# Row turns as whole-array transposes in other groups, with a different home for the row maxima

## The chip, the cores and the metric

The kernel runs on one NeuronCore of one Trainium2 chip. The metric is the device time of that core in microseconds (us). The kernel before takes 3599.44 us, the median of three runs between 3599.09 and 3600.59 us.

The core has five engines with a queue of instructions each. TensorE (PE in the profile, with PEld for its loads of stationary weights) multiplies matrices and writes only to PSUM[...]. VectorE (DVE), ScalarE (ACT) and GpSimd (POOL) work element by element; SyncE (SP) issues most DMAs. An engine takes its queue in order; between engines, semaphores hold an instruction until what it needs is there.

## The reference

One transformer block in float32 with adaptive layer norm, over x of 8 batches x 1024 rows x 256 columns, and then a mixture of 8 experts:

```python
h = _layernorm(x) * (1 + ca) + sa               # ca, sa, ga ...: from c, one row per batch
proj = einsum('bpv,havn->bhapn', h, w_qkv)      # 16 heads of 64: q, k, v
scores = einsum('bhqn,bhkn->bhqk', q, k) / 8
attn = softmax(scores, axis=-1)                 # exact: the row's maximum is subtracted
x = x + ga * (einsum('bhqk,bhkn->bhqn', attn, v) as rows of 1024) @ w_o
h = _layernorm(x) * (1 + cb) + sb
logits = h @ router_w + router_b                # 8 experts
scores = softmax(logits)
G, idx = top_k(scores.T, 512)                   # each expert takes its 512 best rows
eo = relu(h[idx] @ w1 + b1) @ w2 + b2
x = x + gb * scatter_add(eo * G at idx)
```

## The kernel before, in words

**Units and groups.** Attention is cut into 128 units: one batch (8), one pair of heads (8) and one half of the 512 queries (2). A unit's scores stand with keys on the partitions: eight chunks `c` of 128 keys, each a PSUM tile `s` of 128 x 2 x 512 (two banks), made by `scores_mm`. The main loop (line 732) runs in groups `g` of two chunks, four groups to a unit; `gm` is `g % 4`, and this text calls `gm` 0, 1, 2, 3 the first to fourth group. ScalarE copies a chunk to SBUF (`scores_out`, line 376) and VectorE takes the running maximum `top` over chunks (line 381; none for chunk 0, so the first group has one such operation and the others two).

**The maximum of a unit.** At the end of the fourth group `max_turn` (line 383) turns `top` by eight transposes into a tile `tt`, which comes from the same pool of two score tiles, `ps_s`. `split_max` (line 392) reduces it to one negated maximum per query (line 396), and four small VectorE operations (lines 401 to 404) split that into three bf16 parts. They work in `nm`, a corner of `tt` itself: so `tt` is in use until line 404. In the next group `max_rows` turns the parts to rows, and a group later `max_spread` spreads them over all partitions (`less`).

**The lag.** Five groups behind, `subtract` (line 426) adds `less` to a chunk and `exp_of` (line 429) takes the exponential; one group later `values_mm` (line 438) multiplies by v, and GpSimd adds the chunks for the denominator (`add_up`, lines 454 and 457).

**A group's order.** In each group the loop emits: the list "load" of that group (DMAs), in second groups `max_spread`, the subtractions, the two chunks of scores, list "m1" (projections q, k, v, and `max_rows` in first groups), list "post", the exponentials, `values_mm`, `add_up`, in a fourth group `max_turn` and `split_max`, then list "pool" (GpSimd work) and list "m2". Each engine's queue has its part of this order. The lists are filled beforehand by `at(g, list, function, ...)` (line 247).

**One shared bank.** Projections, `max_rows`, denominators and everything in "m2" use one PSUM bank, the tag `mm` of `ps_m`: each user waits for the one before to be evicted.

**The tasks around the change.** For batches 1 to 7, `ln_task` loads 256 rows (four groups ahead), takes statistics (two ahead, list "post", on VectorE), normalises (one ahead, on GpSimd) and turns them in `ln_out` (list "m2"): 8 matmuls against the identity, each with half the array's columns (lines 302 to 309), and two evictions by VectorE (line 311). Batch 0 is turned by 128 x 128 transposes, two at a time, each pair evicted by ScalarE (lines 291 to 301). For each 128 rows of attention's output, `out_proj` multiplies by w_o and `out_add` (VectorE) adds the residual and takes statistics, `out_norm` (GpSimd, next group) normalises; for each pair of these, `out_turn` (line 576) turns 256 rows, again with half-array matmuls (line 585), one ScalarE copy (line 590), `out_route` computes logits, `out_exp` (ScalarE) and `out_score` (VectorE, lines 622 to 626) the softmax over experts, `out_store` stores the rows.

**Where they stand.** `free_slot(g, True)` (line 651) gives the next untaken fourth group, `free_slot(g)` the next untaken group that is neither first nor fourth. `ln_out`, `out_proj` and `out_turn` all take fourth groups: 4, 8 and 4 of the 16 in a batch, so that from unit 20 on each fourth group has one of them behind its `max_turn`. `out_route` then falls in a second group, `out_exp` in the third, `out_score` in the fourth.

The last batch's output (lines 771 to 823) and the experts (from line 826) follow the main loop; only `out_turn` there belongs to the change.

Of the kernel before, what the change touches and what calls it, by code (L numbers as in the profile page):

```python
# [37 lines left out]
P = 128  # L38
# [4 lines left out]
def adaln_block(  # L43
# [29 lines left out]
    scale = 1.0 / N**0.5  # L73
# [4 lines left out]
    ident = const.tile([P, P], F32, name="ident")  # L78
# [17 lines left out]
    modT = const.tile([P, 2 * KC, B], F32, name="modT")  # L96
# [36 lines left out]
    ps_m = attn.enter_context(tc.tile_pool(name="ps_m", bufs=1, space=PSUM))  # L133
# [33 lines left out]
    for i in range(2):  # L167
        t = work.tile([P, NT // 2, D], F32, tag="p", name=f"x_first{i}", bufs=PB)
# [73 lines left out]
    hTs, mods, qks, vs, oTs = {}, {}, {}, {}, {}  # L242
# [4 lines left out]
    def at(g, where, f, *args):  # L247
        steps.setdefault((g, where), []).append((f, args))
# [37 lines left out]
    def ln_out(b, t):  # L286
        if t == 0:
            hTs[b] = work.tile([P, KC, S], F32, tag="hT", name=f"hT{b}")
        xt = ln_x.pop((b, t))[0]
        pt = bank([P, KC, 2 * P], f"ptx{b}_{t}", (b, t) in ((0, 0), (0, 1)))  # L290
        if b == 0:
            for k in range(KC):
                for i in range(2):
                    nc.tensor.transpose(
                        pt[:, k, i * P : (i + 1) * P], xt[:, i, k * P : (k + 1) * P], ident
                    )
                nc.scalar.activation(
                    hTs[b][:, k, 2 * t * P : (2 * t + 2) * P], pt[:, k, :], AF.Identity,
                    bias=modT[:, k, b : b + 1], scale=modT[:, KC + k, b : b + 1],
                )  # L300
            return
        for k in range(KC):
            for i in range(2):
                for m in range(2):
                    c0 = k * P + m * N
                    nc.tensor.matmul(
                        pt[m * N : (m + 1) * N, k, i * P : (i + 1) * P],
                        xt[:, i, c0 : c0 + N], ident, start=True, stop=True,
                    )
        for k in range(KC):  # L310
            nc.vector.tensor_scalar(
                hTs[b][:, k, 2 * t * P : (2 * t + 2) * P], pt[:, k, :],
                modT[:, KC + k, b : b + 1], modT[:, k, b : b + 1],
                op0=ALU.mult, op1=ALU.add,
            )

    def ln_task(b, t, g):
        at(g - 4, "load", ln_load, b, t)
        at(g - 2, "post", ln_stats, b, t)
        at(g - 1, "pool", ln_norm, b, t)  # L320
        at(g, "m2", ln_out, b, t)
# [67 lines left out]
                    turned[u][:, 4 * j + t, :], top[:, j, t * P : (t + 1) * P], ident  # L389
                )  # L390

    def split_max(u):

        tt = turned.pop(u)
        nm = tt[:, :2, :8]
        nc.vector.tensor_reduce(nm[:, 0, :], tt, AX.X, ALU.max, negate=True)  # L396
# [7 lines left out]
        nc.vector.tensor_sub(part[2], rest, part[1])  # L404
# [171 lines left out]
    def out_turn(pool, b, t, tag="mm"):  # L576

        n = f"{b}_{t}"
        pt = pool.tile([P, 2, KC, P], F32, tag=tag, name=f"pth{n}")
        for i in range(2):  # L580
            h2 = o_h[b, t + i]
            for k in range(KC):
                for m in range(2):
                    c0 = k * P + m * N
                    nc.tensor.matmul(
                        pt[m * N : (m + 1) * N, i, k, :], h2[:, c0 : c0 + N], ident,
                        start=True, stop=True,
                    )
# [57 lines left out]
        )  # L646


    taken = set()

    def free_slot(g, behind=False):
        while g in taken or g % 4 == 0 or behind != (g % 4 == 3):
            g += 1
        taken.add(g)
        return g
# [9 lines left out]
    for b in range(B):  # L665
        for p in range(NP):
            P0 = 8 * (b * NP + p)
            for i, g in enumerate((-7, -6, -5, -2)):
                if P0:
                    at(P0 + g, "m1", qk_task, b, p, i)  # L670
            if p % 2 == 0:
                for t, g in enumerate((-9, -3, -1, 5)):
                    if P0 or g > 0:
                        at(P0 + g, "m1", v_task, b, p // 2, t)
            if (b, p) == (B - 1, NP - 1):
                continue

            at(P0 + 17, "load", den_load, b, p)
            at(P0 + 18, "post", den_inv, b, p)
            at(P0 + 19, "load", den_spread, b, p)  # L680
            at(P0 + 20, "pool", den_mul, b, p)
        if b + 1 < B:
            if b + 2 < B:
                for t in range(NT // 2):
                    ln_task(b + 2, t, free_slot(64 * (b + 1) + 39 + 4 * t, True))
            for t in range(NT):
                g = free_slot(64 * (b + 1) + 19 + 4 * t, True)
                at(g - 2, "load", out_load, b, t)
                at(g, "m2", out_proj, ps_m, b, t)
                at(g + 1, "pool", out_norm, b, t)  # L690
                if t % 2:
                    g = free_slot(g + 2, True)
                    at(g, "m2", out_turn, ps_m, b, t - 1)
                    g = free_slot(g + 1)
                    at(g, "m2", out_route, ps_m, b, t - 1)
                    at(g + 1, "post", out_exp, b, t - 1)
                    at(g + 2, "post", out_score, b, t - 1)
                    at(g + 3, "pool", out_store, b, t - 1)
    for u in range(NSU):
        at(4 * u + 4, "m1", max_rows, u)  # L700
        if u < NSU - 1:
# [8 lines left out]
    with tc.manual_schedule():  # L710
# [20 lines left out]
        g = -1  # L731
        while g < 4 * NSU + LAG or steps:
            u, gm = divmod(g, 4)
            run(g, "load")
            if gm == 1 and 0 < u <= NSU:
                max_spread(u - 1)
            u1, gm1 = divmod(g - LAG + 1, 4)
            late = [(u1, 2 * gm1 + i) for i in range(2) if 0 <= u1 < NSU]

            for uc in late[: 1 if gm == 3 else 2]:  # L740
                subtract(*uc)
            if 0 <= u < NSU:
# [24 lines left out]
            run(g, "m2")  # L767
            g += 1


        b = B - 1
# [85 lines left out]
    with tc.tile_pool(name="search", bufs=2) as se, tc.tile_pool(  # L857
        name="pos", bufs=1
    ) as po_, tc.tile_pool(name="se_ps", bufs=2, space=PSUM) as sps, tc.tile_pool(
        name="pos_ps", bufs=1, space=PSUM  # L860
    ) as pps:
        for dst, pattern, mult in (
# [3 lines left out]
            i = po_.tile(list(dst.shape), I32, name=f"i_{dst.name}")  # L866
# [32 lines left out]
        for s in range(15):  # L899
            bit = 28 - 2 * s  # L900
            cnt = se.tile([P, 3], F32, tag="cnt", name=f"cnt{s}")
            for k in range(3):
# [3 lines left out]
                    op0=ALU.is_ge, op1=ALU.add, accum_out=cnt[:, k : k + 1],  # L906
# [226 lines left out]
```

## Time and profile before

| | |
|---|---|
| median of the runs shown | 3599.44 us |
| the profiled execution | 3597.83 us |
| its span, first to last instruction | 3596.1 us |
| mean granted TensorE clock | 0.983 |
| busy: PE / PEld / DVE / ACT / POOL | 96% / 40% / 80% / 68% / 74% |
| PE idle before L367 (scores) | 34.0 us |
| L306, `ln_out`'s half-array matmuls (28 tasks) | 30.6 us busy |
| L585, `out_turn`'s (32 tasks) | 39.2 us busy |
| L388, `max_turn`'s transposes (128 units) | 139.9 us busy |

The page lists, for each line and engine, the count, busy time, mean duration and the idle time of the engine before it. The timeline gives instructions in order of time, runs of the same one merged: start, duration, engine, line, output <- inputs, count, and in brackets the idle time of the engine and what ended it. A float32 matmul stands as two records (two passes), a transpose as one. Ends of matmuls are modelled, and neighbours overlap on the PE; the time that a block takes on the PE is read from its start to the start of the next block.

Attention runs to about 3205 us of the span, the last batch's output and routing to about 3272 us; then come the search for each expert's rows and the experts.

### The profile page before, as it was taken

The page shows a single profiled execution, that of the slowest core. Times are in us where ns is not written, and L with a number is a line of the kernel's source. Part 1 is how long each engine was busy: PE and PEld are TensorE (multiplying, and loading weights), DVE is VectorE, ACT ScalarE, POOL GpSimd, SP SyncE. Part 2 cuts the span into 40 slices and gives each one's busy share as a digit, 9 for nine tenths or more (in the row PEclk, how much of TensorE's full clock was granted, in tenths as well). Part 3 has the DMA queues.
Part 4 walks back from the last instruction along what each step waited for, and adds up shares of the span by engine and source line. Part 5 has one row for each costly group of instructions (what it writes and reads, how often), then busy time and mean ns, then how long its engine had stood idle before and what let it go on. Part 6 is the DMA issues. An engine that isn't in the chain of part 4 may idle for free. (4 is left out here: it accounts for less than half of the span.)

```text
span 3596.1 us, 54368 instructions
## 1 busy us (share of the span) xinstructions
PE 3450.2 (96%) x20718; PEld 1454.7 (40%) x20718; DVE 2859.3 (80%) x3618; ACT 2438.7 (68%) x2996; POOL 2652.1 (74%) x1537
## 2 busy tenths in 40 slices
PE   7999999999999999999999999999999999993898
PEld 3333333343433434334433343344433434442566
DVE  5888888888888888888888888988888888867432
ACT  4777777777777777777777777777777777750111
POOL 2778778888888887978788888887888788752233
PEclk9999999999999999999999999999999999995899
DMA  3020012011130112111211112111211112133342
GB/s 78 13 42 31 25 32 67 30 45 45 51 59 29 50 57 56 34 40 45 66 53 31 48 50 63 31 42 53 59 44 44 41 44 63 46 92 129 93 101 43
DMA packets 189653, 185.40 MB, mean 52 GB/s; under 512 B 48952, under 2 KB 167240, under 8 KB 189264
## 3 DMA queue, kind: packets, MB, share of 16 engines
q1 hardware_dynamic: 173616, 160.29, 16.3%
q0 software_dynamic: 7168, 12.72, 1.8%
q10 hardware_dynamic: 8608, 8.92, 0.8%
q8 instruction: 163, 2.67, 0.3%
q14 instruction: 98, 0.80, 0.1%
HBM read 127.06 MB, written 63.21 MB: 53 GB/s over the span
## 5 line engine op out<-in xcount | busy, mean ns | idle before, releaser
L457 POOL TENSOR_TENSOR acc<-acc,p 128x1024 f32<-128x1024 f32 x762 | 1805.3, 2369 | 362.4 <-ACT p L429 329.1
L376 ACT COPY p<-s 128x1024 f32<-128x1024 f32 x1024 | 995.8, 1018 | 419.1 <-PE s L367 412.1
L426 DVE TENSOR_TENSOR p<-p,less 128x1024 f32<-128x1024 f32 x1024 | 1206.7, 1210 | 32.6 <-PE less L423 30.1
L381 DVE TENSOR_TENSOR top<-top,s 128x1024 f32<-128x1024 f32 x768 | 936.8, 1220 | 276.3 <-ACT p L376 236.0
L429 ACT ACTIVATE p<-p 128x1024 f32<-128x1024 f32 x1024 | 1041.7, 1057 | 73.7 <-DVE p L426 73.3
L367 PE MATMUL s<-qk,qk 64*128 64x512 f32 x4096 | 1024.7, 612 | 34.0 <-DVE parts L404 31.0
L438 PE MATMUL av<-p,v 128*64 128x512 f32 x4096 | 967.2, 593 | 1.8 <-ACT oT L447 1.8
L367 PEld LDWEIGHTS s<-qk,qk 64*128 64x128 f32 x4096 | 358.8, 186 | 527.5 <-issue 240.9
L332 PE MATMUL pq<-hT,wq 128*64 128x512 f32 x2048 | 498.5, 608 | 2.7 <-ACT v L354 2.1
L438 PEld LDWEIGHTS av<-p,v 128*64 128x64 f32 x4096 | 280.6, 137 | 461.4 <-issue 366.2
L454 POOL TENSOR_TENSOR acc<-p,p 128x1024 f32<-128x1024 f32 x127 | 301.6, 2375 | 178.1 <-ACT p L429 178.1
L332 PEld LDWEIGHTS pq<-hT,wq 128*64 128x64 f32 x2048 | 124.8, 136 | 342.2 <-issue 210.8
L349 PE MATMUL pv<-wq,hT 128*64 128x256 f32 x2048 | 249.3, 386 | 0.7 <-ACT qk L337 0.7
L1053 ACT ACTIVATE h<-ph,b_sb 128x512 f32<-128x512 f32 (+1 forms) x72 | 46.0, 639 | 263.5 <-PE ph L1049 263.5
L396 DVE TENSOR_REDUCE tt<-tt 128x8 f32<-128x1024 f32 x128 | 157.4, 1230 | 69.9 <-PE tt L388 69.8
L548 PE MATMUL po<-wo,ot 128*64 128x256 f32 x1792 | 205.7, 382 | 0.0
L349 PEld LDWEIGHTS pv<-wq,hT 128*64 128x64 f32 x2048 | 135.7, 136 | 153.2 <-issue 65.9
L381 DVE TENSOR_TENSOR top<-p,s 128x1024 f32<-128x1024 f32 x128 | 155.8, 1217 | 14.0 <-ACT p L376 14.0
L388 PEld LDWEIGHTS tt<-ident,top 128*128 128x128 f32 x1024 | 109.6, 140 | 106.6 <-DVE top L381 105.8
L519 POOL TENSOR_TENSOR oT<-oT,rb 128x1024 f32<-128x1024 f32 x63 | 150.0, 2380 | 3.7 <-DMA rb<-rden_d 3.7
L548 PEld LDWEIGHTS po<-wo,ot 128*64 128x64 f32 x1792 | 123.5, 137 | 66.1 <-issue 9.4
L388 PE MATMUL tt<-ident,top 128*128 128x128 f32 x1024 | 139.9, 280 | 2.6 <-DVE top L381 2.6
(169 smaller groups left out, 2293.4 us busy)
## 6 DMA issues: line engine op xcount, KB each, us to landing
rb<-rden_d SPq DMA_DIRECT2D x128, 256.0 KB
oT_d<-oT SPq DMA_DIRECT2D x62, 512.0 KB
ot<-oT_d SPq DMA_DIRECT2D x56, 512.0 KB
rows_d<-row SPq DMA_DIRECT2D x64, 132.0 KB
rows_d<-gb_d SPq DMA_DIRECT2D x8, 1024.0 KB
w<-in_L_ffn_w_dram ACTq DMA_DIRECT2D x8, 1024.0 KB
w<-in_L_ffn_w_dram SPq DMA_DIRECT2D x8, 1024.0 KB
lnx<-in_L_attn_inputs_dram SPq DMA_DIRECT2D x28, 256.0 KB
```

Source lines behind the costliest of these rows:

```text
L332: nc.tensor.matmul(pq[m * N : (m + 1) * N, :], wq_of(k, a, 2 * p + m), hTs[b][:, k, sl], start=(k == 0), stop=(k == KC - 1),)
L349: nc.tensor.matmul(pv[m * N : (m + 1) * N, i, :], hTs[b][:, k, t0 : t0 + N], wq_of(k, 2, 4 * g, 4), start=(k == 0), stop=(k == KC - 1),)
L367: nc.tensor.matmul(ps[:, j, :], kt[r, c * P : (c + 1) * P], qt[r, h * QB : (h + 1) * QB], start=True, stop=True,)
L376: nc.scalar.copy(probs[u, c], ps)
L381: nc.vector.tensor_tensor(tops[u], probs[u, 0] if c == 1 else tops[u], ps, ALU.max)
L388: nc.tensor.transpose(turned[u][:, 4 * j + t, :], top[:, j, t * P : (t + 1) * P], ident)
L426: nc.vector.tensor_tensor(probs[u, c], probs[u, c], less[u], ALU.add)
L429: nc.scalar.activation(probs[u, c], probs[u, c], AF.Exp)
L438: nc.tensor.matmul(avs[u][j * N : (j + 1) * N, :], v[:, c, hh * N : (hh + 1) * N], pT[:, j, :], start=(c == 0), stop=(c == NT - 1),)
L454: nc.gpsimd.tensor_tensor(sums[u], pts[0], pts[1], ALU.add)
L457: nc.gpsimd.tensor_tensor(sums[u], sums[u], pt, ALU.add)
L548: nc.tensor.matmul(po[m * N : (m + 1) * N, :], ot[:, p, m * N : (m + 1) * N], wo[:, p, :], start=(p == 0), stop=(p == NP - 1),)
```

## The change

- `ln_out` uses one path for all batches: four 128 x 128 transposes into the bank, then two ScalarE evictions. For batch 0 all four transposes now stand ahead of both evictions; for the others half-array matmuls and VectorE evictions are gone.
- `out_turn` uses four transposes too.
- `split_max(u, busy)`: where the fourth group has an `out_proj` behind it (the set `covered`, 56 of 128 units), `nm` stays in `tt`. In the other 72, `nm` is a tile of the shared bank `mm`.
- `ln_out` moves to third groups, 30, 34, 42 and 46 of the batch before (with its load, statistics and normalisation moving along: the statistics stand in first groups 28, 32, 40, 44). `out_proj` stands in fourth groups 19, 23, 31, 35, 43, 47, 55, 59; `out_turn` three groups after the second of a pair (third groups), `out_route` six after (second), `out_exp` seven after (third), `out_score` nine after (first), `out_store` ten after (second).

```diff
@@ ln_out
-        if b == 0:
-            for k in range(KC):
-                for i in range(2):
-                    nc.tensor.transpose(...)
-                nc.scalar.activation(...)
-            return
         for k in range(KC):
             for i in range(2):
-                for m in range(2):
-                    c0 = k * P + m * N
-                    nc.tensor.matmul(
-                        pt[m * N : (m + 1) * N, k, i * P : (i + 1) * P],
-                        xt[:, i, c0 : c0 + N], ident, start=True, stop=True,
-                    )
+                nc.tensor.transpose(
+                    pt[:, k, i * P : (i + 1) * P], xt[:, i, k * P : (k + 1) * P], ident
+                )
         for k in range(KC):
-            nc.vector.tensor_scalar(
-                hTs[b][:, k, 2 * t * P : (2 * t + 2) * P], pt[:, k, :],
-                modT[:, KC + k, b : b + 1], modT[:, k, b : b + 1],
-                op0=ALU.mult, op1=ALU.add,
+            nc.scalar.activation(
+                hTs[b][:, k, 2 * t * P : (2 * t + 2) * P], pt[:, k, :], AF.Identity,
+                bias=modT[:, k, b : b + 1], scale=modT[:, KC + k, b : b + 1],
             )
@@ split_max
-    def split_max(u):
+    def split_max(u, busy):
         tt = turned.pop(u)
-        nm = tt[:, :2, :8]
+        nm = tt[:, :2, :8] if busy else ps_m.tile([P, 2, 8], F32, tag="mm", name=f"nm{u}")
         nc.vector.tensor_reduce(nm[:, 0, :], tt, AX.X, ALU.max, negate=True)
@@ out_turn
-                for m in range(2):
-                    c0 = k * P + m * N
-                    nc.tensor.matmul(
-                        pt[m * N : (m + 1) * N, i, k, :], h2[:, c0 : c0 + N], ident,
-                        start=True, stop=True,
-                    )
+                nc.tensor.transpose(pt[:, i, k, :], h2[:, k * P : (k + 1) * P], ident)
@@ the lists
-        ln_task(1, t, free_slot(39 + 4 * t, True))
...
-            if b + 2 < B:
-                for t in range(NT // 2):
-                    ln_task(b + 2, t, free_slot(64 * (b + 1) + 39 + 4 * t, True))
+            for t in range(NT // 2):
+                ln_task(b + 1, t, 64 * b + (30, 34, 42, 46)[t])
             for t in range(NT):
-                g = free_slot(64 * (b + 1) + 19 + 4 * t, True)
+                g = 64 * (b + 1) + 19 + 4 * (t + t // 2)
+                covered.add(g)
                 at(g - 2, "load", out_load, b, t)
                 at(g, "m2", out_proj, ps_m, b, t)
                 at(g + 1, "pool", out_norm, b, t)
                 if t % 2:
-                    g = free_slot(g + 2, True)
-                    at(g, "m2", out_turn, ps_m, b, t - 1)
-                    g = free_slot(g + 1)
-                    at(g, "m2", out_route, ps_m, b, t - 1)
-                    at(g + 1, "post", out_exp, b, t - 1)
-                    at(g + 2, "post", out_score, b, t - 1)
-                    at(g + 3, "pool", out_store, b, t - 1)
+                    at(g + 3, "m2", out_turn, ps_m, b, t - 1)
+                    at(g + 6, "m2", out_route, ps_m, b, t - 1)
+                    at(g + 7, "post", out_exp, b, t - 1)
+                    at(g + 9, "post", out_score, b, t - 1)
+                    at(g + 10, "pool", out_store, b, t - 1)
@@ the main loop
-                split_max(u)
+                split_max(u, g in covered)
```

More of the change, by code (lines that the diff above doesn't have):

```diff
@@ L290, in ln_out @@
         pt = bank([P, KC, 2 * P], f"ptx{b}_{t}", (b, t) in ((0, 0), (0, 1)))
-        if b == 0:
-            for k in range(KC):
-                for i in range(2):
-                    nc.tensor.transpose(
-                        pt[:, k, i * P : (i + 1) * P], xt[:, i, k * P : (k + 1) * P], ident
-                    )
-                nc.scalar.activation(
-                    hTs[b][:, k, 2 * t * P : (2 * t + 2) * P], pt[:, k, :], AF.Identity,
-                    bias=modT[:, k, b : b + 1], scale=modT[:, KC + k, b : b + 1],
-                )
-            return
         for k in range(KC):
             for i in range(2):
-                for m in range(2):
-                    c0 = k * P + m * N
-                    nc.tensor.matmul(
-                        pt[m * N : (m + 1) * N, k, i * P : (i + 1) * P],
-                        xt[:, i, c0 : c0 + N], ident, start=True, stop=True,
-                    )
+                nc.tensor.transpose(
+                    pt[:, k, i * P : (i + 1) * P], xt[:, i, k * P : (k + 1) * P], ident
+                )
         for k in range(KC):
-            nc.vector.tensor_scalar(
-                hTs[b][:, k, 2 * t * P : (2 * t + 2) * P], pt[:, k, :],
-                modT[:, KC + k, b : b + 1], modT[:, k, b : b + 1],
-                op0=ALU.mult, op1=ALU.add,
+            nc.scalar.activation(
+                hTs[b][:, k, 2 * t * P : (2 * t + 2) * P], pt[:, k, :], AF.Identity,
+                bias=modT[:, k, b : b + 1], scale=modT[:, KC + k, b : b + 1],
             )
@@ L582, in out_turn @@
             for k in range(KC):
-                for m in range(2):
-                    c0 = k * P + m * N
-                    nc.tensor.matmul(
-                        pt[m * N : (m + 1) * N, i, k, :], h2[:, c0 : c0 + N], ident,
-                        start=True, stop=True,
-                    )
+                nc.tensor.transpose(pt[:, i, k, :], h2[:, k * P : (k + 1) * P], ident)
         h2T = small.tile([P, 2, KC, P], F32, tag="h2T", name=f"h2T{n}", bufs=1)
@@ L646, in last_load @@
         )
[L649 to L655, printed above, removed]
+    covered = set()
     for t in range(NT // 2):
         at(-1 if t < 2 else 0, "m1", ln_out, 0, t)
-        ln_task(1, t, free_slot(39 + 4 * t, True))
     for i, g in ((0, -1), (2, -1), (1, 0), (3, 1)):
```

## The prediction

> **What bounds the kernel.** First the page's engine line and its row for scores:
>
> ```profile
> PE 3450.2 (96%) x20718; PEld 1454.7 (40%) x20718; DVE 2859.3 (80%) x3618; ACT 2438.7 (68%) x2996; POOL 2652.1 (74%) x1537
> L367 PE MATMUL s<-qk,qk 64*128 64x512 f32 x4096 | 1024.7, 612 | 34.0 <-DVE parts L404 31.0 <-DVE top L381 2.2 <-ACT qk L337 0.7
> ```
>
> Then busy time by stretches (length; PE, PEld, DVE, ACT, POOL, count in brackets; clock, DMA):
>
> ```profile
> 1000.00:1500.00 500.00, 497.77 (x3005) 199.49 (x3002) 430.90 (x521) 373.06 (x455) 415.29 (x239) 1.00 0.18 48
> ```
>
> TensorE is the bound through attention: 497.8 of 500 us at full clock, and nearly all that it waits for is line 404, the last of the small operations that hold `tt`. So PE time counts in full, and so does how `tt` is released. The timeline shows that twice. With nothing behind `max_turn`:
>
> ```profile
> 362.68 1.09 PE L388 MATMUL tt<-ident,top 128*128 128x128 f32 x8
> 363.70 1.13 PE L367 MATMUL s<-qk,qk 64*128 64x512 f32 x4
> 363.81 1.23 DVE L396 TENSOR_REDUCE tt<-tt 128x8 f32<-128x1024 f32 x1 [0.68 <-PE tt L388]
> 365.74 0.19 DVE L404 TENSOR_TENSOR parts<-tt,parts 128x8 bf16<-128x8 f32 x1
> 366.08 1.13 PE L367 MATMUL s<-qk,qk 64*128 64x512 f32 x4 [1.25 <-DVE parts L404]
> ```
>
> and with `ln_out` behind it:
>
> ```profile
> 267.77 1.09 PE L388 MATMUL tt<-ident,top 128*128 128x128 f32 x8
> 268.79 1.09 PE L306 MATMUL ptx<-ident,lnx 128*64 128x128 f32 x16
> 269.81 1.13 PE L367 MATMUL s<-qk,qk 64*128 64x512 f32 x4
> 270.83 0.19 DVE L404 TENSOR_TENSOR parts<-tt,parts 128x8 bf16<-128x8 f32 x1
> 271.16 1.13 PE L367 MATMUL s<-qk,qk 64*128 64x512 f32 x4 [0.22 <-DVE parts L404]
> ```
>
> The second score tile starts 3.40 us after `max_turn` began without `ln_out` and 3.39 with it: **the turn in the fourth group is free now**, it fills a wait. The same holds behind `out_turn`. Behind `out_proj` (3.60 us on the PE) there is no wait.
>
> **The skill.** "TensorEngine Tiling (Array Packing)", Restrictions: column tiling switches off the float32 transpose mode. The trace agrees: L306 has 16 records for 8 matmuls, L388 one each. Same page, Key Properties: changing the tiling mode drains the array. I read 0.15 us between `max_turn`'s last regular slot and the next block, against either neighbour, so the change of shape costs no more than before. "SBUF — State Buffer", SBUF: two separate sides: VectorE and GpSimd share a port pair as an exclusive lock held for a whole instruction. The trace agrees (below). "PSUM — Partial Sum Buffer", PSUM bank collisions: engines must be kept apart by bank; so moving `nm` to another bank is what allows TensorE to write `tt`'s bank while the small operations run.
>
> **The change, part by part**, against the profiled execution's 3597.8 us.
>
> 1. Earlier release. In 72 units the reduction is `tt`'s last reader. It ends at 363.81 + 1.23 = 365.04, and the wait takes 0.15 us (365.93 to 366.08), so the second tile could start at 365.19 in place of 366.08: 0.89 us earlier. It still waits 0.63 (a tile takes 0.86, half of the 1.92 from one score block to the next block). `max_rows` needs line 404 and could start at 366.05; after this tile (1.06 us in the trace to the next block) it starts at 366.25, so it doesn't take the wait over. `nm` waits for `mm`'s last user, a projection evicted about 2 us before. 16 units have nothing behind `max_turn` today (0 to 8 and 13 to 19, before the fourth groups fill): 16 x 0.89 = 14.2 us gained.
>
> 2. Turns moved. In 28 + 28 fourth groups a free turn goes away and an equal number stands in third groups, where nothing waits: it costs its whole PE time. The trace has no four full-speed transposes; it has eight, 1.02 us to the next block, 0.109 each plus 0.15. So four take between 0.51 (half) and 0.59 (the gap whole); I take 0.59. Per unit: 0.89 gained, 0.59 paid, 0.30 net; 56 x 0.30 = 16.8 us, at most 4.5 more.
>
> 3. Batch 0's turns. Each second pair of transposes waits 0.66 us or more for the eviction of the first. In group 0 one round trip of about 0.8 us goes; in the prologue some 0.4, as the second turn waits for its rows as well. 1.2 us gained (0 to 3).
>
> 4. The last batch's four `out_turn`s: 1.12 us become about 0.65 in a cycle through GpSimd, TensorE, ScalarE and VectorE, where VectorE waits 1.2 to 1.6 us for the logits each time: 4 x 0.45, 1.7 us gained (0 if the cycle has slack that I don't see).
>
> 5. ScalarE takes 56 evictions of 0.57 us (its row for batch 0's), VectorE loses 56 of 0.535. They stand behind the third group's exponentials and ahead of the fourth group's copies. In the timeline around 262.25, where the fourth group's scores start, the exponentials end 0.89 us after that start. The transposes put the start 0.59 later, so the evictions run from 0.30 to 1.33 after it; the first copy starts at 1.24 today, and `max_turn` has 0.5 us to spare; the projection wants `mm` at 1.92. With `out_exp` in the same group (30 and 42; today's pattern around 599.03) all is 0.38 later, 1.71, and with 0.15 for the wait just in time. So it hides; without that cover it is up to 0.3 us x 12, and I take 0.6 in all.
>
> 6. VectorE in first groups. It now has `out_score` there and, moved from second groups, the statistics. The timeline after an `out_proj`:
>
> ```profile
> 610.67 0.18 DVE L117 BATCH_NORM_AGGREGATE mv_b<-st_b 128x2 f32<-128x6 f32 x1
> 610.77 2.32 DVE L426 TENSOR_TENSOR p<-p,less 128x1024 f32<-128x1024 f32 x2
> 613.00 1.22 DVE L381 TENSOR_TENSOR top<-p,s 128x1024 f32<-128x1024 f32 x1
> 614.01 0.73 POOL L573 TENSOR_TENSOR row<-row,mod 128x256 f32<-128x256 f32 x1
> 614.23 2.35 DVE L426 TENSOR_TENSOR p<-p,less 128x1024 f32<-128x1024 f32 x2
> 616.50 2.54 DVE L381 TENSOR_TENSOR top<-top,s 128x1024 f32<-128x1024 f32 x2
> 619.34 1.99 PE L367 MATMUL s<-qk,qk 64*128 64x512 f32 x8
> ```
>
> VectorE has no gap from 610.77 on. What is inserted at 614.2 delays the maxima, and the third group's second score tile (due 619.34 + 0.86 = 620.20) needs the second of them (619.04, plus 0.15): 1.0 us of slack. `out_score` takes 0.4 to its first multiplication, which then wants the shared port; the lock shows here:
>
> ```profile
> 604.63 4.79 POOL L457 TENSOR_TENSOR acc<-acc,p 128x1024 f32<-128x1024 f32 x2 [0.30 <-ACT p L429]
> 605.30 1.85 DVE L626 TENSOR_SCALAR row<-ex,rd 128x8 f32<-128x8 f32 x2
> ```
>
> the pair (0.22 each when free) waited for the running GpSimd addition. In its new place it arrives at 614.54 and L573 ends at 614.74: 0.2 us of wait, `out_score` about 0.8. The statistics take 1.17 (L116 0.41 and L117 0.18, twice, overlapping). So `out_score` ends at 614.95, the statistics at 616.1, and the subtraction of 614.23 starts at about 616.03: 1.8 late, less 1.0 of slack: 0.8. Behind it on VectorE wait the two maxima, and for them TensorE's second tile. It happens in groups 32 and 44 of batches 1 to 6: 12 x 0.8 = 9.6 us lost. `out_score` alone (16 groups) fits the slack: 0. Statistics alone (16): 0.1 each, 1.6.
>
> 7. GpSimd. Normalising stands in second groups. In group 45 it stands behind `out_norm` (3.8 us from its start), a `den_mul` (2.38), two additions (4.8) and `out_store` (0.4); it needs 3.5 and ends some 0.5 us after the transposes of group 46 want it: 6 x 0.5 = 3 us. Elsewhere 1.5 us or more are left. SP: each load of rows still stands two groups (10 us or more) ahead of its statistics, and each of `out_load` two ahead of its `out_proj`; in front of the moved loads in SP's queue stand the stores of `den_mul` and of the denominators from the group or two before, which are through by then; the load for group 34 goes out just ahead of the 1 MB of `gates`, not behind it. 0.
>
> Sum: -14.2 - 16.8 - 1.2 - 1.7 + 0.6 + 9.6 + 1.6 + 3.0 = **-19.1 us**, profiled 3578.7 us. The median of the runs shown is 1.6 us above the profiled execution: 3580.3 us. What a measurement can tell from no change is 0.2%, 7.2 us.
>
> **Rivals.** (a) *The lock goes the other way.* The margin in part 6 is 0.2 us. If the multiplication comes just after GpSimd has begun its next instruction, it waits 2.4 us instead of 0.2. The 12 heavy groups lose 2.2 more each (26), the other 16 with `out_score` 0.8 + 2.2 - 1.0 = 2.0 each (32): 58 us, 3638 us, slower. It decides once 19.1/58, a third of these groups, miss. For it: both sides hang on the same event (L117's end), so all would miss together. Against: today's phase, read twice in the trace, is the other one.
> (b) *The release gives nothing*, as another reader or `max_rows` holds the second tile to line 404's time. Then 72 x 0.89 = 64 us are missing: 3644 us. Against: 0.2 us are left for `max_rows`.
> (c) *VectorE's delay is swallowed*, since it has lost 30 us of evictions: parts 6 and 7 cost nothing: 3566 us. Against: those evictions didn't stand in these stretches.
> (d) *The backlog is only partly worse* (stalls of 1.5 to 2.5 us in the heavy groups, some with ScalarE): within 7 us of today, 3592 to 3606.
>
> **How the numbers follow.** Forecast 0.58 (own range 3571 to 3592), (c) 0.15, (d) 0.12, (a) 0.10, (b) 0.05. Faster: 0.58 less a few hundredths, plus 0.15: 0.71; same 0.13; slower 0.16. The range reaches from just below (c), 3562, to just above (d), 3608: about 8 in 10.
>
> **What would show it.** L306 and L585's half-array rows gone, transposes in their place with four records a task; PE idle before scores charged to the reduction, some 0.6 us x 72 = 45 us, and none to the small operations but in covered units; VectorE's old eviction row gone and 64 ScalarE evictions of 0.56 us; PE waits on the running maximum of about 0.8 us in third groups 34 and 46, 12 of them. Wrong if the multiplications of `out_score` average near 1.2 us or more in first groups (rival a), or if the second tile still starts 3.4 us after `max_turn`.

## The result: slower, and the profile after

The changed kernel takes 3636.02 us (median of five runs, 3635.27 to 3640.91), the kernel before on the same chip 3599.09 us: a ratio of 1.0105, 95% interval 1.0093 to 1.0117. The forecast of 3580.3 us was wrong in size and in sign, and 3636 lies outside its range of 3562 to 3608. The profiled executions' spans are 3633.5 and 3596.1 us, at mean granted clocks of 0.981 and 0.983.

The page after has the engines' row and the row for scores like this (L352 is L367 of before):

```profile
PE 3440.9 (95%) x19998; PEld 1424.7 (39%) x19998; DVE 2847.5 (78%) x3562; ACT 2469.2 (68%) x3052; POOL 2650.9 (73%) x1537
L352 PE MATMUL s<-qk,qk 64*128 64x512 f32 x4096 | 1036.2, 616 | 75.5 <-DVE top L366 51.1
```

TensorE has 720 records fewer and is busy 9 us less. But it waits 75.5 us before scores in place of 34.0, and two thirds of that is for the running maximum, which stood at 2.2 us before. The list of waits gives the two parts (total, times, longest):

```profile
PE s L352 <- DVE top L366: 51.1, 56, 2.8
PE s L352 <- DVE nm L382: 23.4, 70, 0.3
```

**What came as forecast.** The timeline of a unit with nothing behind `max_turn`:

```profile
354.18 1.09 PE L373 MATMUL tt<-ident,top 128*128 128x128 f32 x8
355.20 1.13 PE L352 MATMUL s<-qk,qk 64*128 64x512 f32 x4
355.38 1.23 DVE L382 TENSOR_REDUCE nm<-tt 128x8 f32<-128x1024 f32 x1 [0.76 <-PE tt L373]
356.67 1.13 PE L352 MATMUL s<-qk,qk 64*128 64x512 f32 x4 [0.33 <-DVE nm L382]
357.31 0.20 DVE L390 TENSOR_TENSOR parts<-nm,parts 128x8 bf16<-128x8 f32 x1
```

The second score tile starts when the reduction has ended (356.61), and no longer after L390. From the start of `max_turn` it is 2.49 us in place of 3.40. Block by block, the wait inside the first group's scores is 0.61 us (1.52 before, 0.50 behind a half-array turn). Four transposes in a third group take 0.585 us to the next block.

**What took the time.** Read from block to block, attention from group 8 to group 511 lasts 36.3 us longer. Groups 5 and 6, 33 and 34, 45 and 46, 57 and 58 of a batch, the two behind each `out_score`, are together 71.3 us longer. Of this, 8.2 us are fourteen turns that now stand in groups 34 and 46, at 0.585 us each, which leaves 63.1 (the expectations below have 64); TensorE's idle time in these groups has gone from 0.7 to 50.4 us. All other groups are together 34.9 us shorter. As in the prediction, the places behind groups 32 and 44, which have the statistics too, are called heavy here, and those behind groups 4 and 56 light. The timeline of a heavy one (first group 44, from 761.0 on group 45):

```profile
759.09 0.73 POOL L559 TENSOR_TENSOR row<-row,mod 128x256 f32<-128x256 f32 x1
759.23 0.16 DVE L603 TENSOR_REDUCE rd<-ex 128x2 f32<-128x16 f32 x1
759.43 0.17 DVE L604 RECIPROCAL rd<-rd 128x2 f32<-128x2 f32 x1
759.63 2.54 DVE L607 TENSOR_SCALAR row<-ex,rd 128x8 f32<-128x8 f32 x2
759.78 4.83 POOL L443 TENSOR_TENSOR acc<-acc,p 128x1024 f32<-128x1024 f32 x2
762.09 2.34 DVE L412 TENSOR_TENSOR p<-p,less 128x1024 f32<-128x1024 f32 x2
764.35 2.53 DVE L366 TENSOR_TENSOR top<-top,s 128x1024 f32<-128x1024 f32 x2
765.61 1.13 PE L352 MATMUL s<-qk,qk 64*128 64x512 f32 x4 [1.10 <-DVE top L366]
766.93 1.13 PE L352 MATMUL s<-qk,qk 64*128 64x512 f32 x4 [0.19 <-DVE top L366]
```

`out_score` begins 0.14 us into `out_norm`'s last addition L559, as the forecast had it, and its first multiplication starts 0.19 us before that addition ends. But the pair takes 2.54 us. Instruction by instruction, the first takes 0.23 us and the second 2.40: the running addition L443 starts on GpSimd 13 ns after the second multiplication, and both end within 0.03 us of each other. Behind it wait the subtractions, the maxima, and then TensorE.

All 64 of these instructions (minimum, median, maximum in ns), first before and then after:

```profile
L626 DVE TENSOR_SCALAR row<-ex,rd x64: 217/228/1998, 605.3 to 3270.8; 128x8 f32<-128x8 f32 x64
```
```profile
L607 DVE TENSOR_SCALAR row<-ex,rd x64: 219/255/2412, 599.9 to 3307.5; 128x8 f32<-128x8 f32 x64
```

Before, nearly every first multiplication took about 1.7 us, some 1.5 of them waiting, and every second took 0.22. After, it is the other one of the pair: 27 of the 28 second multiplications for batches 0 to 6 take 2.39 to 2.41 us. The wait has grown only from 1.5 to 2.2 us, but it has moved to a place without slack.

**What the stalls cost besides.** A part of the loss is TensorE's clock. The timeline of a heavy place in batch 1, and the busy time of TensorE in a stretch behind the stall (length; PE; clock, DMA):

```profile
686.29 1.13 PE L352 MATMUL s<-qk,qk 64*128 64x512 f32 x4 [2.15 <-DVE top L366]
687.61 1.84 PE L352 MATMUL s<-qk,qk 64*128 64x512 f32 x4 [0.20 <-DVE top L366]
689.39 2.87 PE L317 MATMUL pq<-hT,wq 128*64 128x512 f32 x8
```
```profile
687.90:691.30 3.40, 3.40 (x10) 0.50 0.02 7
```

For 3.41 us the granted clock is half, and the score tile takes 1.84 us in place of 1.13. This happens behind 5 of the 12 stalls of the heavy places and behind a longer one in batch 7; a group 34 or 46 with such a stretch is 1.5 to 1.65 us longer than one without, some 8 us in all. In the traces of all twelve kernels, each of the 19 half-clock stretches between groups 8 and 511 stands behind a wait of TensorE of at least 2.1 us (there are 27 such waits), and none behind a wait of 0.9 to 1.6 us. What decides between waits of the same length isn't shown.

### The profile page after: what moved, and what is told of

The parts are those of the page before. It is cut to its first block, busy times and chain, and to the rows that moved or that the text cites. A ratio compares the mean times of both kernels' runs of the same rounds, so it can differ in the third digit from the quotient of the medians.

```text
span 3633.5 us, 53046 instructions
## 1 busy us (share of the span) xinstructions
PE 3440.9 (95%) x19998; PEld 1424.7 (39%) x19998; DVE 2847.5 (78%) x3562; ACT 2469.2 (68%) x3052; POOL 2650.9 (73%) x1537
## 5 line engine op out<-in xcount | busy, mean ns | idle before, releaser
L443 POOL TENSOR_TENSOR acc<-acc,p 128x1024 f32<-128x1024 f32 x762 | 1804.8, 2368 | 436.4 <-ACT p L415 405.7
L352 PE MATMUL s<-qk,qk 64*128 64x512 f32 x4096 | 1036.2, 616 | 75.5 <-DVE top L366 51.1
L352 PEld LDWEIGHTS s<-qk,qk 64*128 64x128 f32 x4096 | 354.8, 187 | 544.8 <-DVE top L366 208.4
L324 ACT COPY qk<-pq 128x512 f32<-128x512 f32 x128 | 74.9, 585 | 102.5 <-PE pq L317 102.5
```

What stands on the lines that cost most here:

```text
L352: nc.tensor.matmul(ps[:, j, :], kt[r, c * P : (c + 1) * P], qt[r, h * QB : (h + 1) * QB], start=True, stop=True,)
L443: nc.gpsimd.tensor_tensor(sums[u], sums[u], pt, ALU.add)
```

## The experiments

Medians in us, each with its ratio to the kernel before on the same chip. All edits but that of e4 (from the kernel before) start from the changed kernel; e7 adds to e6 and e10 to e7.

| run | median (range) | ratio, 95% interval |
|---|---|---|
| the change | 3636.02 (3635.27 to 3640.91) | 1.0105 [1.0093, 1.0117] |
| e1_one_mul_moved | 3615.75 (3614.65 to 3617.15) | 1.0049 [1.0032, 1.0066] |
| e2_score_fourth | 3585.99 (3581.24 to 3586.76) | 0.9965 [0.9953, 0.9978] |
| e3_stats_second | 3618.22 (3617.96 to 3619.64) | 1.0054 [1.0038, 1.0071] |
| e4_turns_only | 3595.47 (3594.27 to 3600.17) | 0.9992 [0.9984, 1.0001] |
| e5_gap | 3583.11 (3581.47 to 3586.02) | 0.9957 [0.9940, 0.9974] |
| e6_mul_scalar_late | 3574.40 (3574.15 to 3574.59) | 0.9932 [0.9916, 0.9949] |
| e7_best | 3572.67 (3571.70 to 3576.18) | 0.9929 [0.9912, 0.9945] |
| e8_nm_in_tt | 3697.49 (3696.91 to 3698.26) | 1.0274 [1.0257, 1.0292] |
| e9_independent | 3583.59 (3582.03 to 3585.84) | 0.9957 [0.9941, 0.9974] |
| e10_norm_earlier | 3574.53 (3571.52 to 3576.15) | 0.9932 [0.9915, 0.9948] |

My theory after the two traces: the second multiplication's wait for the shared port is the loss. The rival: VectorE has simply too much to do in these first groups, with or without the lock.

### One multiplication on ScalarE (e1)

```diff
             row = o_h[b, t + i]
-            nc.vector.tensor_scalar_mul(row[:, D:], ex[:, i, :], den[:, i : i + 1])
+            if i == 0:
+                nc.vector.tensor_scalar_mul(row[:, D:], ex[:, i, :], den[:, i : i + 1])
+            else:
+                nc.scalar.mul(row[:, D:], ex[:, i, :], den[:, i : i + 1])
```

> The changed kernel with the second multiplication of out_score alone moved to ScalarE. Theory A (in first groups the first multiplication gets the port as GpSimd's addition ends, the second finds GpSimd's next instruction begun and waits 2.4 us, and VectorE's delay stalls the score tiles of the third group): the light cases (groups 4 and 56) lose nothing any more, the heavy ones (32 and 44) some 0.7 us instead of 3.1; 64 us of stalls become about 9, the time about 3581 us. Rival B (VectorE has simply too much work in first groups, lock or not): one operation of 0.22 us less in 28 groups, at most 6 us gained, about 3630 us. Rival C (ScalarE's evictions or GpSimd's normalising are late): no change or a little slower, 3636 to 3640 us.

3615.75: neither number. Its timeline at the same place:

```profile
755.17 0.23 DVE L608 TENSOR_SCALAR row<-ex,rd 128x8 f32<-128x8 f32 x1
755.23 0.30 ACT L610 ACTIVATE row<-ex,rd 128x8 f32<-128x8 f32 x1 [1.78 <-DVE rd L604]
755.31 2.34 DVE L412 TENSOR_TENSOR p<-p,less 128x1024 f32<-128x1024 f32 x2
755.44 1.98 ACT L415 ACTIVATE p<-p 128x1024 f32<-128x1024 f32 x2
757.33 0.35 ACT L467 COPY den<-pd 128x256 f32<-128x256 f32 x1
757.73 1.94 PE L317 MATMUL pq<-hT,wq 128*64 128x512 f32 x8 [1.27 <-ACT den L467]
```

VectorE's wait is gone: the subtraction follows the first multiplication at once, and scores wait for the running maximum 2.9 us in all (51.1 in the changed kernel). But ScalarE takes its queue in order, and its multiplication stands ahead of the exponentials: it waits 1.78 us for the reciprocal, the exponentials and the copy that frees `mm` come late, and TensorE waits 1.27 us for that bank. The list of waits has this under projections of v and of q and k:

```profile
PE pv L334 <- ACT den L467: 16.8, 13, 1.6
PE pq L317 <- ACT den L467: 16.5, 13, 1.3
```

The edit exchanged one wait for another, and it has a second cost at the end: everything behind group 511 lasts 422.7 us, 412.5 in the changed kernel. There ScalarE issues the loads of the experts' weights, and the last batch's multiplication on ScalarE starts 8.4 us late behind them; GpSimd and TensorE wait for it. Less the 33.3 us and these 10, e1 would be near 3572 where the theory had 3581, but waits don't simply add up. The run shows that VectorE's wait goes with the second multiplication; it leaves open what that wait alone costs.

### `out_score` in fourth groups (e2), statistics in second groups (e3)

```diff
-                    at(g + 9, "post", out_score, b, t - 1)
+                    at(g + 8, "post", out_score, b, t - 1)
```

> The changed kernel with out_score one group earlier, in fourth groups, three of four of them ahead of an out_proj. Theory A: those three hide as in the kernel before, the heavy groups keep the statistics alone (0.2 us each); the fourth (group 3 of a batch, nothing behind max_turn) delays the reduction by some 1.5 us, 7 x 1.5 = 10 us. About 3584 us. Rival B' (the statistics in first groups are the cause, not out_score): the stalls in groups 32 and 44 stay near 3 us, about 3620 us. Rival C: no change.

```diff
-        at(g - 2, "post", ln_stats, b, t)
+        at(g - 1, "post", ln_stats, b, t)
```

> The changed kernel with ln_stats one group later, in second groups behind that group's maxima. Theory A: the heavy groups become light ones, 1.7 us instead of 3.1 twelve times: 17 us gained, about 3619 us; groups 4 and 56 stay at 1.7 us. Rival B' (statistics are the cause): the stalls go, about 3572 us.

e2: 3585.99, e3: 3618.22, both the theory's numbers. In e2 the waits in groups 5, 33, 45 and 57 are gone; in a fourth group the first multiplication takes 1.5 to 1.7 us and the second 0.22, as in the kernel before. A new wait of 1.3 us stands in group 4, six times. In e3 the heavy groups' stall in groups 33 and 45 falls from 2.24 to 1.18 us, the light ones' stays. So the statistics deepen the stall, by some 18 us in all; behind the shorter stalls of its heavy places the clock stays whole, which is a part of the 18. But the stall goes with `out_score` and is there without the statistics.

### What lets the second multiplication in (e5, e9)

In the kernel before, GpSimd's next addition depended on the one just ended and started 78 ns after its end. In the changed kernel the next one is independent, and its record starts about 43 ns before the other's end. e5 puts a copy of one element per partition between them that reads what was just written; e9 does the same with a copy that reads a constant; its edit is shown against e5 (`tiny` is a new tile of 128x1, its allocation left out).

```diff
             nc.gpsimd.tensor_tensor(oT, oT, dens.pop((b, p)), ALU.mult)
+            nc.gpsimd.tensor_copy(tiny, oT[:, :1])
...
         nc.gpsimd.tensor_add(h2, h2, mods[b][:, 1, :])
+        nc.gpsimd.tensor_copy(rs, h2[:, :1])
```

> The changed kernel with one added GpSimd copy of 128x1 behind the last addition of each out_norm and behind each den_mul's product, which reads the result just written. Theory A1 (VectorE gets the port between two GpSimd instructions only where the second must wait for the first's result; otherwise GpSimd's next one has it first): the second multiplication of out_score slips in ahead of the copy, takes 0.22 us instead of 2.4; stalls fall from 64 us to about 10, about 3581 us. Theory A2 (GpSimd's next instruction always comes first, or the long addition takes the port in spite of the copy): no change, 3636 us, or about 0.2 us per copy longer.

```diff
-            nc.gpsimd.tensor_copy(tiny, oT[:, :1])
+            nc.gpsimd.tensor_copy(tiny, ones[:, :1])
...
-        nc.gpsimd.tensor_copy(rs, h2[:, :1])
+        nc.gpsimd.tensor_copy(tiny, ones[:, :1])
```

> Edit: like e5_gap, a copy of one element per partition on GpSimd after the last addition of out_norm and after den_mul, but reading a constant, so that it does not depend on the instruction before it. Theory (dependency): VectorE's second multiplication gets the shared port only where GpSimd's next instruction waits for the result of the one before it; here it does not, so the copy starts directly behind the addition, the running addition of the denominator directly behind the copy, and the second multiplication still waits about 2.4 us (perhaps the first comes through in place of it, or neither): 3634 to 3645 us. Rival (length): any short instruction between is enough to let VectorE in: both multiplications at 0.22 to 0.4 us and 3583 us as in e5_gap.

e5: 3583.11, e9: 3583.59. The timeline of e5 in group 44, then that of e9:

```profile
756.85 0.73 POOL L561 TENSOR_TENSOR row<-row,mod 128x256 f32<-128x256 f32 x1
757.37 0.37 DVE L610 TENSOR_SCALAR row<-ex,rd 128x8 f32<-128x8 f32 x2
757.65 0.18 POOL L562 COPY rs_b<-row 128x1 f32<-128x1 f32 x1
757.78 4.83 POOL L444 TENSOR_TENSOR acc<-acc,p 128x1024 f32<-128x1024 f32 x2
762.19 1.99 PE L353 MATMUL s<-qk,qk 64*128 64x512 f32 x8
```
```profile
756.81 0.73 POOL L561 TENSOR_TENSOR row<-row,mod 128x256 f32<-128x256 f32 x1
757.34 0.36 DVE L610 TENSOR_SCALAR row<-ex,rd 128x8 f32<-128x8 f32 x2
757.48 0.18 POOL L562 COPY tiny<-ones 128x1 f32<-128x1 f32 x1
757.62 4.84 POOL L444 TENSOR_TENSOR acc<-acc,p 128x1024 f32<-128x1024 f32 x2
757.62 2.34 DVE L413 TENSOR_TENSOR p<-p,less 128x1024 f32<-128x1024 f32 x2
```

Both multiplications together take 0.37 us, and the two score tiles of group 45 in e5 follow without a wait between them. e5 is the clean measure of the loss: the multiplications stay where they are, GpSimd even has more to do, and 52.7 us come back (3636.02 less 3599.09, against 3583.11 less 3598.89). They hold the clock's part too: no half-clock stretch is left between groups 8 and 511. The rival is out as the cause of these; what VectorE's work alone costs, with the lock out, is 0.5 us at each heavy place in e5.

e9 took a part of my theory with it. I had put the difference down to the dependence, and expected 3634 or more. But the copy that depends on nothing starts where L443 started in the changed kernel, and the multiplication isn't held. What e5 and e9 have in common is the distance to GpSimd's next *large* instruction, counted from the start of the second multiplication. The table has the pairs of attention that have one close by:

| kernels | next large GpSimd instruction starts | second multiplication takes |
|---|---|---|
| the change, e3 | 1 to 21 ns after it | 2.39 to 2.41 us |
| e8, 21 pairs | 6 to 19 ns after | 2.40 to 2.41 us |
| e8, 6 pairs (the first takes 2.40 us here) | 136 to 138 ns after | 0.22 us |
| before, e2, e4 | 128 to 137 ns after | 0.22 us |
| e9 | 127 to 142 ns after | 0.22 us |
| e5 | 253 to 259 ns after | 0.22 us |

A gap is enough, whether a dependence or a short copy makes it. Where between 21 and 127 ns the border lies wasn't tried, nor what sets it.

### Both multiplications where they disturb nothing (e6)

```diff
         nc.vector.reciprocal(den, den)
+        o_x[b, t] = ex, den
+        if b == B - 1:
+            out_mul(b, t)
+
+    def out_mul(b, t):
+        ex, den = o_x.pop((b, t))
         for i in range(2):
             row = o_h[b, t + i]
-            nc.vector.tensor_scalar_mul(row[:, D:], ex[:, i, :], den[:, i : i + 1])
+            if b == B - 1:
+                nc.vector.tensor_scalar_mul(row[:, D:], ex[:, i, :], den[:, i : i + 1])
+            else:
+                nc.scalar.mul(row[:, D:], ex[:, i, :], den[:, i : i + 1])
...
                     at(g + 9, "post", out_score, b, t - 1)
+                    at(g + 10, "post", out_mul, b, t - 1)
```

> The changed kernel with both multiplications of out_score on ScalarE, one group later (second groups, between the projection's eviction and the exponentials), so that ScalarE doesn't wait for the reciprocal. Theory A: VectorE's stalls go but for the heavy groups (0.4 + 1.17 - 1.0 = 0.6 us, 12 times): about 3580 us. Rival B (too much work in first groups, lock or not): half of the 64 us at most, 3605 us or more. If, as with one multiplication moved inside the first group, 1.2 us stand in all 28 groups at ScalarE's denominator copy again, that wait was not from the reciprocal.

3574.40. ScalarE's queue at this place:

```profile
756.75 0.59 ACT L324 COPY qk<-pq 128x512 f32<-128x512 f32 x1 [0.74 <-PE pq L317]
757.23 0.49 ACT L616 ACTIVATE row<-ex,rd 128x8 f32<-128x8 f32 x2
757.62 1.99 ACT L415 ACTIVATE p<-p 128x1024 f32<-128x1024 f32 x2
```

What was wrong in e1 was the place, not the engine: a group later the reciprocal is long there, and the multiplications wait for nothing. The last batch's stay on VectorE, so the wait at the end of e1 is gone as well. e6 is 8.7 us below e5. In the profiled executions 5.5 us of the difference lie in attention, nearly all at the heavy places, as the multiplications leave VectorE's full stretch too. Another 2.9 lie ahead of group 8, where the first projections ran slower in e5 (granted clock 0.76 from 28 to 35 us, 1.00 in e6); the edit touches nothing there. The 0.6 us that the theory left at each heavy place came to 0.1: the slack there is larger than the 1.0 us of the prediction.

### The turns alone (e4), and `nm` always in `tt` (e8)

e4 gives the kernel before the new bodies of `ln_out` and `out_turn`, and leaves the lists and `split_max` as they are. e8 is:

```diff
-                split_max(u, g in covered)
+                split_max(u, True)
```

> The kernel before with the new bodies of ln_out and out_turn alone (four transposes, evictions by ScalarE), everything in its old group and nm in tt. Theory: a turn behind max_turn fills a wait that lasts until the small operations are through, so half a turn saves nothing there; the start of the kernel gains some 2 us: 3597 us. Rival (TensorE's saved time counts in full): 56 x 0.44 = 24 us less, 3575 us.

> The changed kernel with nm in tt in all units: the early release alone undone. Theory: 72 x 0.89 = 64 us more, less 2.3 at the start: about 3698 us. Rival (the release gives nothing, something else holds the second tile): 3634 to 3640 us.

e4: 3595.47, with an interval that includes no change at all (a ratio of 1). Its wait for the small operations, and then that of e8:

```profile
PE s L352 <- DVE parts L389: 63.4, 70, 1.3
```
```profile
PE s L352 <- DVE parts L390: 87.2, 70, 1.3
PE s L352 <- DVE top L366: 44.4, 46, 2.8
```

In e4 the turns are half as long on TensorE and the wait behind them has grown from 31.0 to 63.4 us: a turn in a fourth group was free, and a shorter one gives nothing. e8, 3697.49 us, is 61.5 us above the changed kernel, as expected. From group 8 to 511 each of 70 first groups behind a released unit is 0.91 us longer, 0.89 forecast, 63.7 us in all; the start is 2.4 us shorter, for the reason shown under e7.

### Statistics later and the start mended (e7), normalising earlier (e10)

e7 is e6 with the edit of e3 and

```diff
-    covered = set()
+    covered = {3}
```

> The same with ln_stats in second groups and the fourth group of unit 0 counted as covered (nm in tt there, as mod_rows wants the shared bank behind it). Theory: no stall in third groups, 7 us less than with the multiplications moved alone, and 2.3 us less at the start: about 3571 us, faster than both kernels. If normalising on GpSimd now comes too late for the transposes, third groups 30 to 46 show waits for it, up to 1 us each, 28 times.

3572.67, not to be told from e6, and 0.71% faster than the kernel before. The 7 us of the statistics couldn't come, since e6 had lost no more than 0.1 us at each heavy place; the start is 2.2 us shorter, as expected. In the changed kernel the first unit's `nm` is in `mm` with work of the prologue behind it. TensorE's timeline of the start, the changed kernel's:

```profile
53.59 1.09 PE L373 MATMUL tt<-ident,top 128*128 128x128 f32 x8
57.01 1.88 PE L224 MATMUL pr<-wm,sT 128*8 128x512 f32 x4 [2.33 <-issue]
58.82 1.56 PE L352 MATMUL s<-qk,qk 64*128 64x512 f32 x6
```

L224 needs `mm`, which `nm` holds until L390. In e7 L224 follows `max_turn` after 1.03 us in place of 3.42. The wait that stays is 0.85 us in group 46 from block to block (up to 0.6 of it idle), six times. e10 moves load, statistics and normalisation of those rows one group earlier:

```diff
-        at(g - 4, "load", ln_load, b, t)
+        early = 1 if t == 3 and b > 1 else 0
-        at(g - 1, "post", ln_stats, b, t)
-        at(g - 1, "pool", ln_norm, b, t)
+        at(g - 4 - early, "load", ln_load, b, t)
+        at(g - 1 - early, "post", ln_stats, b, t)
+        at(g - 1 - early, "pool", ln_norm, b, t)
```

> Edit: e7_best with the load, statistics and normalisation of the rows turned in groups 46 (batches 1 to 6) one group earlier; the transposes stay in group 46. Theory (GpSimd's backlog in group 45 holds up the transposes of group 46 by 0.85 us, 6 times): those waits go, 3567 to 3569 us against 3572.7. Rival: out_norm, normalisation and the additions of group 44 together run over into group 45, den_mul and the denominator's additions come as much later, and the wait moves to another place: 3572 us or more.

3574.53, with a range that covers most of e7's: nothing was gained, as the rival had it. In the lists of waits, the first line is e7's and the second e10's:

```profile
PE ptx L293 <- POOL lnx L281: 3.8, 6, 0.6
```
```profile
PE less L410 <- DVE p L413: 4.7, 6, 0.8
```

The turn of group 46 no longer waits for GpSimd, and group 48 now waits for VectorE's subtraction, as often and about as long. I didn't follow what makes that subtraction late.

## Why the prediction was wrong, point by point

- **Part 1, the release:** right. 2.49 us from `max_turn` to the second tile where 2.51 was worked out; e8 measures the release at 0.91 us a unit, against 0.89.
- **Part 2, the turns moved:** right. Four transposes cost 0.585 us, 0.59 taken; and e4 confirms that the turns had been free where they stood. Parts 1 and 2 together were put at 31.0 us; 70 units at 0.91 less 56 turns at 0.585 are 30.9, and the units at either end aren't in that count.
- **Part 3, batch 0's turns:** the gain is there and of the size forecast. From the first transpose to the projection behind the turns, the prologue takes 3.75 us (3.95 before) and group 0 takes 3.93 (4.98 before): 1.25 us. Group 1's scores start 2.1 us earlier, but what goes beyond the turns is clock: the projection ahead of them took 3.26 us before (granted clock 0.76 from 28 to 35 us) and 1.94 after (1.00), and 3.45 in e5, which has the same turns. All of it is lost by group 4, which starts at 58.82 us, 58.86 before: L224 waits 2.4 us more for `mm`. I had looked at `mm`'s user ahead of `nm`, and not at the one behind it.
- **Part 4, the last batch:** nothing of the 1.7 us came. The four turns there wait longer for GpSimd: 14.1 us in the list of waits, 11.9 before. e4, with only the turns changed, shows it as well (13.9). So the cycle had the slack that the part's zero end allowed for.
- **Part 5, ScalarE's evictions:** right as far as the trace can tell. TensorE's waits for `hT` come to 3.3 us after and 4.6 before.
- **Part 6 is the step that failed.** The first half was met closely: the multiplication arrives 0.19 us before `out_norm`'s addition ends, 0.2 forecast, and gets through. But I priced the pair as one event, a wait of 0.2 and then two free multiplications. By the time of the second, GpSimd is at its next instruction, and the second has to get the port anew. The pair read before (1.85 us for two) had been taken as "wait, then both free", without asking why the second was free: GpSimd's next addition there depended on the one before, which left a gap. Behind `out_norm` and `den_mul` GpSimd's next instruction doesn't depend on the one before, and there is no gap. "SBUF — State Buffer" of the Trainium skill, SBUF: two separate sides, gives the port pair to whichever starts first, for the whole instruction. If the start is read from the records, this case doesn't agree: in the table's first row the second multiplication's record starts 1 to 21 ns before GpSimd's, and it is the one that waits. Measured at the heavy places of batches 1 to 6: 2.25 us in the group behind `out_score` and 0.46 in the next, together 2.7 where 0.8 was put. At five of these twelve the halved clock adds some 1.6, which the prediction did not have at all. At the light places it was about 1.67 where 0 was put.
- **Part 7, GpSimd's normalising:** the right place and mechanism. The wait in group 46 is 0.7 to 0.85 us once the lock is out of the way (e5 to e7; 0.54 in e9), 0.5 forecast; e10 shows that the same time is lost elsewhere if it is moved.
- **The sum, with the lock out:** e5 and e9 stand at 3583.1 and 3583.6 us, 3 us above the forecast of 3580.3. Attention isn't what is missing. In e5's profiled execution it is 18.2 us shorter than before from group 8 to 511, where parts 1, 2, 5, 6 and 7 come to 16.2; the waits of parts 6 and 7 are 11.1 us, 14.2 forecast. What is missing lies at the ends, in the places of parts 3 and 4: the start is 2.6 us longer, with the wait of L224 and the lower clock in it, and what follows group 511 is 1.5 us longer, which varies by more than that between the runs (410.6 to 414.4 us without e1).
- **Rival (a)** had the time (3638) and the stalls (3.0 and 2.0 us a group) but not quite the mechanism: it let the *first* multiplication come too late. I gave it 0.10, as both sides of that meeting hang on one event and the phase was read twice. The phase held; the next meeting, one instruction later, was not on the list. Rivals (b) and (c) are out: e8 separates the release, and VectorE's delay reaches TensorE. (d) asked for 1.5 to 2.5 us in the heavy groups; they have 2.7, and over 4 with the clock halved. That the time came so near to that of (a) is in part luck: its stalls lack the clock, and its light ones are too long.

## What to carry to other kernels

When a small operation is moved next to a stream of GpSimd additions, each of its instructions that uses the shared port has to get the port anew: look at what GpSimd starts when *that* one wants in, and whether GpSimd's next instruction follows without a gap. A wait costs nothing where slack covers it (before, 1.5 us at each place, and free); in a place without slack, 2.2 us of wait cost TensorE 1.7 us (light) to 2.2 us (heavy, 2.7 less the 0.5 of e5), and more where the clock fell behind it. So a step is moved with its waits and not with its busy time. If an operation only needs to be done some time later, put it where its operands are long there: the same multiplication on ScalarE cost some 1.3 us of TensorE's time at each place in e1 and none in e6.

## What the runs showed of the hardware

- Two of the denominator's additions in a row on GpSimd are 78 or 79 ns apart (end to start) where the second uses the first one's result (365 pairs of the changed kernel's attention). Where `out_norm`'s last addition, a `den_mul` and these additions follow each other without such a dependence, the second's record starts 31 to 64 ns before the first's end.
- A multiplication of VectorE whose record starts 1 to 21 ns ahead of a large GpSimd instruction waits for the whole of it, 2.4 us; with 127 ns it takes its usual 0.22 us. Which record starts first doesn't decide it.
- A GpSimd copy of one element per partition doesn't hold up such a multiplication: in e9 the records overlap by up to 0.18 us and take 0.18 and 0.22 us. In e5, where they overlap by about 0.09 us, they take the same.
- TensorE's granted clock fell to half for 3.41 us behind 19 of 27 waits of 2.1 us or more in attention, and behind none of 0.9 to 1.6 us.
